# Two fused layers on one core: the first norm worked on the spectrum, image loads moved into room the scans leave, spectral matrices built beside the last image, a norm's factor by logarithm and exponential

## The chip, the cores and the metric

The kernel runs on one core of one Trainium2 chip. The metric is the time on the device, in microseconds, of one execution; the median of several runs is given, with the lowest and the highest. The profile is of one further execution. A core has several engines with an instruction stream each: PE (TensorE, matrix products into PSUM), DVE (VectorE), ACT (ScalarE, table functions), POOL (GpSimd) and SP (SyncE, used here to start transfers; ACT can start them too). They run side by side and wait for one another by semaphores. SBUF is the memory on the core with 128 partitions, PSUM the one that PE writes to, DRAM the memory outside.

## The reference, cut to what matters

The input `x` has the shape (4, 48, 48, 128): four images of 48 by 48 with 128 channels. Two layers are applied, each as a group norm, an inner function and a residual:

```python
x = x + _L0_conv_ref(_gn(x), ...)     # selective scan in four directions
x = x + _L1_conv_ref(_gn(x), ...)     # attention with Fourier layers
```

Inside layer 0, after a projection, a 3 by 3 convolution per channel and a SiLU, this runs for four directions of each image, over 2304 positions, 256 channels and 16 states:

```python
h = h * exp(dt_l * A) + (dt_l * u_l) * B_l
y = einsum('bkdn,bkn->bkd', h, C_l)
...
y = (y - mu) * rsqrt(var + 1e-05) * norm_g + norm_b      # layer norm over channels
y = y * silu(z);  out = einsum('bhwd,cd->bhwc', y, out_proj_w)
```

Layer 1 sees the group-normed result as 4 x 48 single pictures of 48 by 128 (a batch of 4, 48 time steps T; H is 48, W the 128 channels). Its first step is an instance norm of every picture (mean and variance over H and W). Keys, queries and values are each a spectral convolution of that (a real 2-d Fourier transform, a product with learned weights on the low frequencies, the inverse) plus a skip; 32 heads attend over the 48 time steps; then come a projection with a spectral convolution, two more instance norms, and two spectral layers `wM0` and `wM1`, with a GELU between them.

## The kernel before, in words

**Layer 0** (`layer0`, from line 53). The 128 partitions hold channels, in two halves (`NF` = 2). Four images, four directions in the order 0, 2, 1, 3, five chunks each (four of 480 positions, one of 384) and 16 states make 1280 steps. A step is spread over the engines by a table of lags (`LAGS`, line 544), and every instruction in it goes through `on.`, which keeps the order in which the program was written on each engine. In a step PE copies B's row to all partitions (`pb`), DVE multiplies it with `du` (`db`, in three of four states; in the fourth POOL does it from a row that SP has loaded, `bbc`), ACT makes `da` by two exponentials, DVE runs the scan (`h`), POOL multiplies by C (`hc`, whose rows SP loads two states at a time as `cbc`), and PE adds `hc` up over the states (`yp`). ACT carries the last state of a chunk to the next (`carry`).

Once per step `piece()` (line 528) hands out one piece of side work: the projection of the next direction (`project`), the projection and convolution of the next image (`front`, started in the third chunk of an image's first direction, and by none in the last image), or the end of a chunk (`back`, lines 343 to 390). `back` is one of this for every chunk of an image's last direction: 20 in all, of which the last stands behind the last scan. It subtracts the mean over channels, squares (ACT), sums (PE, `pv`), takes the square root (ACT) and the reciprocal (DVE) for the factor `rs`, makes the gate `z` (PE, ACT's Identity and SiLU), multiplies (POOL), projects (PE, `po` and `pr`) and writes the chunk of x1 to DRAM:

```python
on.scalar.activation(rs[:, 0:n], pv[:, 0:n], AF.Sqrt, bias=eps)          # L363
...
    if f == 0:
        on.vector.reciprocal(rs[:, 0:n], rs[:, 0:n])                     # L371
...
on.vector.tensor_mul(xo[:, 0:n], po[:, 0:n], rs[:, 0:n])                 # L381
```

**Layer 1** (`layer1`, from line 642). Instructions written with `nc.` are placed by the framework's scheduler in each engine's order; those with `on.` keep the written order. The stages:

1. x1 is read back as `xa`, four images side by side on the free axis (L744). Weights for values and projection become `dgt` in DRAM (L762 to 793), every head's block 16 times over. `spectral_weights` (948 to 979) makes two sets of 32 matrices of 96 by 96 from `wM0` and `wM1` and two constant Fourier matrices: POOL multiplies (`wih`), PE multiplies (`psw`), ACT copies to one buffer (`spw`), SP stores to DRAM (`sp_d`).
2. Group-norm statistics (ACT copies a block, DVE's bn_stats reads the copy), the affine on all of `xa` (L999), then `first_norm` (695 to 719): the mean by 48 entries of 384 columns on PE with a 128 by 128 matrix of constants (`pm_in`), the subtraction on DVE and POOL, squares on ACT, the variance on PE (`pv_in`), the factor `r`.
3. `prepare` (823 on) makes selectors, and the products of query and key weights (`w_q`, `w_k`, `g_qk`) from some 90 small loads on SP. `forward_w` (721 to 734) transforms along W, multiplies by `r` on the way out of PSUM, and writes `da_x` to DRAM, from which `load_a2` (736) reads it with H on the partitions. PE transposes the pictures (`xnt`) and applies selectors (`psel`, `pplain`, L1041 to 1057).
4. Scores and softmax (L1119 to 1171).
5. Attention times values (L1219 to 1276): for two pairs of images and four groups k of frequencies, three slices q of time steps and four groups g of heads. SP loads `xrep` (16 transfers of 16 partitions for each q, L1227) and `grep` from `dgt` (one transfer for each g, at q = 0, L1235); ACT copies a part of `grep` to PSUM (`gp`), DVE and POOL multiply (`v`, `v3`), PE sums up (`acc`). Buffers: four of `grep` (pool `pg`, L1183), two of `xrep`, `v` and `v3` (pool `p2`, L1182).
6. The rest of layer 1 in two interleaved strands (`Strand`, from 1341), which read `sp_d` back.

Of the kernel before, what the change touches and what calls it, by code (L numbers as in the profile page):

```python
# [53 lines left out]
def layer0(ctx, tc, io, x1_dram):  # L54
# [14 lines left out]
    small = ctx.enter_context(tc.tile_pool(name="l0_small", bufs=2))  # L69
    ps_s = ctx.enter_context(tc.tile_pool(name="l0_pss", bufs=1, space=PSUM))  # L70
    ps_b = ctx.enter_context(tc.tile_pool(name="l0_psb", bufs=1, space=PSUM))
    ps_a = ctx.enter_context(tc.tile_pool(name="l0_psa", bufs=1, space=PSUM))
# [207 lines left out]

    def load_dt(b, k):
        w_dt = two.tile([32 + R, D], F32, tag="w_dt", name=f"w_dt{b}_{k}")
        nc.sync.dma_start(w_dt[32 : 32 + R], io["dt_proj_wT"][k])
        return w_dt
# [58 lines left out]
    def back(b, s, n, yb, x, w, wb):  # L343
# [19 lines left out]
        on.scalar.activation(rs[:, 0:n], pv[:, 0:n], AF.Sqrt, bias=eps)  # L363
        for f in range(NF):
# [5 lines left out]
            if f == 0:  # L370
                on.vector.reciprocal(rs[:, 0:n], rs[:, 0:n])  # L371
# [214 lines left out]
    for j, chunks in enumerate(directions):  # L586
# [9 lines left out]
        for m, c in enumerate(chunks):  # L596
            c.carry = carries[j % 2]
            for i in range(N):
                if k == ORDER[0] and b + 1 < B and m > 1 and coming is None and not any(g in later for g in backs):
                    coming = front(b + 1, images[b + 1])  # L600
                    later.append(coming)
                if i in (N // 2 + 3, N // 2 + 6):
# [13 lines left out]
    while later:  # L616
        piece()

# [24 lines left out]
def layer1(ctx, tc, io, x1_dram, out):  # L643
# [5 lines left out]
    nc = tc.nc  # L649
    img = ctx.enter_context(tc.tile_pool(name="l1_img", bufs=1))  # L650
    const = ctx.enter_context(tc.tile_pool(name="l1_const", bufs=1))
    small = ctx.enter_context(tc.tile_pool(name="l1_small", bufs=2))
    dram = ctx.enter_context(tc.tile_pool(name="l1_dram", bufs=1, space=DRAM))
# [9 lines left out]

    ident = load("ident1", [128, 128], io["c_ident"])
    gmat = load("gmat1", [128, 128], io["c_group"])
    fw = load("fw", [128, 66], io["c_FW"])
    fh = load("fh", [96, 96], io["c_FH"])
    fhi = load("fhi", [96, 96], io["c_FHI"])
    ih = load("ih", [96, 96], io["c_IH"])
    eps = const.tile([128, 1], F32, name="eps1")  # L670
    nc.gpsimd.memset(eps, 1e-5)
    mean_m = const.tile([128, 128], F32, name="mean_m")
    nc.gpsimd.memset(mean_m, 1.0 / (H * W))
    n_g = everywhere("n_g", io["L1_norm_g"], 6)
# [3 lines left out]

    turn = [0]

    def either():
        turn[0] += 1
        return nc.gpsimd if turn[0] % 3 == 0 else nc.vector
# [8 lines left out]
    def per_image(t, n=HB):  # L692
        return t[:, None, :].to_broadcast([128, n, BT])

    def first_norm(psum, work, x):

        pm = psum.tile([128, 512], F32, tag="st", name="pm_in")
        for q in range(H // 2):
            nc.tensor.matmul(pm[:, 0 : 2 * BT], mean_m, x[:, 2 * q : 2 * q + 2], start=(q == 0), stop=(q == H // 2 - 1))  # L699
        m = small.tile([128, BT], F32, tag="in_m", name="in_m")  # L700
        nc.scalar.copy(m, pm[:, 0:BT])
        nc.vector.tensor_add(m, m, pm[:, BT : 2 * BT])
        pv = psum.tile([128, 512], F32, tag="st", name="pv_in")
        for q in range(0, H, HB):
            d = x[:, q : q + HB]
            either().tensor_sub(d, d, per_image(m))
            sq = work.tile([128, HB, BT], F32, tag="blk", name=f"sq_{q}")
            nc.scalar.activation(sq, d, AF.Square)
            for j in range(0, HB, 2):
                nc.tensor.matmul(  # L710
                    pv[:, 0 : 2 * BT], mean_m, sq[:, j : j + 2], start=(q + j == 0), stop=(q + j == H - 2)
                )
        r = small.tile([128, BT], F32, tag="in_r", name="in_r")
        nc.scalar.copy(r, pv[:, 0:BT])
        nc.vector.tensor_add(r, r, pv[:, BT : 2 * BT])
        nc.scalar.activation(r, r, AF.Sqrt, bias=eps)
        nc.vector.reciprocal(r, r)
        nc.vector.tensor_scalar(r, r, n_g[:, 0:1], None, ALU.mult)
        return r

    def forward_w(psum, work, src, r, name):


        da = dram.tile([2, 33, H, BT], F32, name=f"da_{name}")
        for q in range(0, H, HB):
            a = work.tile([66, HB, BT], F32, tag="blk", name=f"a_{name}{q}")
            for j in range(0, HB, 2):
                p = psum.tile([128, 512], F32, tag="mm", name=f"pa_{name}{q}_{j}")
                nc.tensor.matmul(p[0:66, 0 : 2 * BT], fw, src[:, q + j : q + j + 2], start=True, stop=True)
                nc.vector.tensor_mul(  # L730
                    a[:, j : j + 2], p[0:66, 0 : 2 * BT].rearrange("p (a t) -> p a t", t=BT), per_image(r, 2)[0:66]
                )
            nc.sync.dma_start(da.rearrange("c k h t -> (c k) h t")[:, q : q + HB], a)
        return da
# [7 lines left out]
    xa = img.tile([128, H, BT], F32, name="xa")  # L742
    for b in range(B):
        dmas[b % 2].dma_start(xa[:, :, b * T : (b + 1) * T], x1_dram[b])  # L744

    pair_t = [img.tile([128, H, 128], F32, tag=f"p{p}", name=f"xnt{p}") for p in range(2)]
    sp_d = [dram.tile([96, 32, 96], F32, name=f"sp_d{i}") for i in range(2)]
# [4 lines left out]
    dgt = dram.tile([4, NH, 16, 3 * NC], F32, name="dgt")  # L752
    with ExitStack() as pw:
# [30 lines left out]
        for k in range(4):  # L784
            gt = q1.tile([NH, 3, NC], F32, name=f"gtt{k}")
            for c in range(3):
# [4 lines left out]
            nc.sync.dma_start(  # L791
                dgt[k], gt.rearrange("h c n -> h (c n)")[:, None].to_broadcast([NH, 16, 3 * NC])
            )
# [29 lines left out]
    def prepare():  # L823
# [30 lines left out]

        cqk = pe.tile([T, NH], F32, name="cqk")
        nc.vector.tensor_mul(cqk, ws_q[0:T], ws_k[0:T])
# [975 lines left out]
```

## Time and profile before

| what | us |
|---|---|
| median of 3 runs (lowest, highest) | 5088.06 (5079.85, 5090.88) |
| profiled execution, its time | 5084.95 |
| profiled execution, its span | 5083.1 |
| DVE busy in the span | 4225.4 (83%) |
| PE busy | 4214.9 (83%) |
| POOL busy | 4033.8 (79%) |
| ACT busy | 2911.3 (57%) |

In the profile "L50" is the line of the helper that records all `on.` instructions, so those groups are told apart by their tiles. A group's line gives engine, operation, output and inputs with their sizes (partitions x elements), the count, then the busy time in us and the mean of one in ns, then the idle time of the engine just before them and what ended it. In the chain of work that ended last each row is a start, a length and what it was; "issue" is time in which nothing in the profile was waited for, and a q behind an engine's name (SPq, ACTq) is its sequencer, which starts transfers. Stretches of the span in this case: layer 0 ends with the issue of its last x1 write at 4213.10, the scores start at 4411.76, attention times values runs from about 4547 to 4810, and the strands begin at 4812.36.

### The profile page before, as it was taken

How to read it: one execution, taken by the hardware profiler on the slowest of the kernel's cores; microseconds unless marked ns; L12 is line 12 of the kernel's file. 1: busy time of each engine (PE TensorE's matmuls, PEld its weight loads, DVE VectorE, ACT ScalarE, POOL GpSimd, SP SyncE). 2: the span in 40 equal slices, each digit the busy share in tenths (PEclk: the TensorE clock that was granted, in tenths of full speed). 3: DMA queues.
4: the chain of work that ended last, by engine and by line, in shares of the span. 5: the costliest groups of instructions: out<-in, count | busy, mean ns of one | idle time of the engine just before them, and what ended most of it. 6: DMA issues, size and time to landing. Idle time of an engine off the chain costs nothing. (4 is left out here: it accounts for less than half of the span.)

```text
span 5083.1 us, 44364 instructions
## 1 busy us (share of the span) xinstructions
PE 4214.9 (83%) x12344; PEld 1897.5 (37%) x12344; DVE 4225.4 (83%) x2908; ACT 2911.3 (57%) x6446; POOL 4033.8 (79%) x2219
## 2 busy tenths in 40 slices
PE   6889898888798988887989888878787785888876
PEld 2334333333343333333433333333333332453343
DVE  3689998989899989898999898999999983356536
ACT  3666566666565666665656666656656552223334
POOL 4589998988899989798999898899999872346531
PEclk9989999999899999998999999999899986989977
DMA  1223233323233333232333332333233226236546
GB/s 54 72 88 101 93 113 92 101 91 96 93 107 105 104 93 100 88 99 92 106 103 107 91 102 84 99 105 103 99 104 94 93 71 127 64 81 176 166 99 152
DMA packets 276767, 509.25 MB, mean 100 GB/s; under 512 B 100602, under 2 KB 185434, under 8 KB 276326
## 3 DMA queue, kind: packets, MB, share of 16 engines
q1 hardware_dynamic: 265318, 502.61, 32.8%
q10 hardware_dynamic: 11200, 3.81, 0.5%
q8 instruction: 97, 1.59, 0.1%
q14 instruction: 152, 1.25, 0.1%
HBM read 462.58 MB, written 43.72 MB: 100 GB/s over the span
## 5 line engine op out<-in xcount | busy, mean ns | idle before, releaser
L50 POOL TENSOR_TENSOR hc<-h,cbc 128x960 f32<-128x960 f32 (+1 forms) x1280 | 2719.2, 2140 | 461.9 <-DVE h L50 337.4
L50 DVE TENSOR_TENSOR_SCAN h<-da,carry,db 128x961 f32<-128x961 f32 (+1 forms) x1280 | 2702.3, 2130 | 121.2 <-ACT carry L50 86.8
L50 ACT ACTIVATE da<-dt,a_neg 128x480 f32<-128x480 f32 (+1 forms) x2560 | 1661.2, 649 | 1247.4 <-DVE h L50 1201.6
L50 PE MATMUL yp<-hc,ident 128*128 128x480 f32 (+1 forms) x5120 | 2279.6, 573 | 6.8 <-POOL hc L50 6.6
L50 PEld LDWEIGHTS yp<-hc,ident 128*128 128x128 f32 x5120 | 1008.0, 199 | 1428.5 <-issue 1022.4
L50 DVE TENSOR_TENSOR db<-du,pb 128x960 f32<-128x960 f32 (+1 forms) x960 | 1063.1, 1107 | 210.6 <-PE pb L50 155.5
L50 PE MATMUL pb<-bs,pick 112*128 112x480 bf16 (+1 forms) x960 | 360.6, 376 | 400.9 <-DVE db L50 399.2
L50 POOL TENSOR_TENSOR db<-du,bbc 128x960 f32<-128x960 f32 (+1 forms) x320 | 688.5, 2152 | 0.0
L50 PE MATMUL pc<-pad,cdiag 128*128 128x480 f32 (+1 forms) x630 | 283.2, 561 | 9.0 <-ACT pad L50 9.0
L1248 POOL TENSOR_TENSOR v<-grep,xrep 128x768 f32<-128x768 f32 x96 | 174.2, 1821 | 111.2 <-PE acc L1252 64.0
L50 POOL TENSOR_TENSOR du<-dt,xc 128x480 f32<-128x480 f32 (+1 forms) x160 | 204.9, 1281 | 37.1 <-ACT dt L50 37.1
L1252 PE MATMUL acc<-v,attn_c 128*64 128x384 f32 x1152 | 212.8, 511 | 25.8 <-POOL v L1248 15.8
L1244 DVE TENSOR_TENSOR v<-gp,xrep 128x1536 f32<-128x1536 f32 x96 | 165.3, 1754 | 82.4 <-PE acc L1252 36.2
L50 PE MATMUL px<-xc,w_xp 128*112 128x480 f32 (+1 forms) x320 | 215.6, 761 | 17.0 <-ACT xc L50 13.3
L50 ACT COPY db<-carry 128x1 f32<-128x1 f32 x1280 | 226.0, 177 | 5.4 <-DVE db L50 2.1
L50 PEld LDWEIGHTS <-pick 112*128 112x128 bf16 x960 | 97.9, 102 | 331.8 <-issue 307.6
L50 ACT ACT_TABLE_LOAD x146 | 187.3, 1283 | 25.5 <-PE gv_g L50 13.8
L50 PE MATMUL pd<-xd,w_dt 8*128 8x480 f32 (+1 forms) x320 | 167.9, 605 | 38.6 <-ACT bs L50 24.6
L50 ACT COPY carry<-h 128x2 f32<-128x2 f32 x1024 | 192.7, 188 | 0.0
L50 PEld LDWEIGHTS pc<-pad,cdiag 128*128 128x128 f32 x630 | 121.9, 194 | 142.3 <-issue 114.8
L50 PE MATMUL yp<-y,ident 128*128 128x480 f32 (+1 forms) x240 | 166.4, 823 | 0.2
L1252 PEld LDWEIGHTS acc<-v,attn_c 128*64 128x64 f32 x1152 | 88.2, 141 | 146.6 <-issue 63.4
(367 smaller groups left out, 3183.2 us busy)
## 6 DMA issues: line engine op xcount, KB each, us to landing
cbc<-cd SPq DMA_DIRECT2D x512, 480.0 KB
bbc<-cd SPq DMA_DIRECT2D x256, 240.0 KB
cbc<-cd SPq DMA_DIRECT2D x128, 384.0 KB
xrep<-dxt SPq DMA_DIRECT2D x384, 72.0 KB
grep<-dgt SPq DMA_DIRECT2D x32, 576.0 KB
bbc<-cd SPq DMA_DIRECT2D x64, 192.0 KB
dgt<-gtt SPq DMA_DIRECT2D x4, 2304.0 KB
x<-in_xT SPq DMA_DIRECT2D x16, 288.0 KB
```

The costliest lines, as they stand in the source:

```text
L50: return lambda *args, **kw: self._tc.keep_in_program_order(emit(*args, **kw))
L1244: nc.vector.tensor_mul(v, gp[:, None, :, 0:NC].to_broadcast([128, 2, 2, NC]), x[:, :, 0:2])
L1248: nc.gpsimd.tensor_mul(v3, r[:, 2:3].to_broadcast([128, 2, NC]), x[:, :, 2])
L1252: nc.tensor.matmul(acc[c][64 * b : 64 * b + 64, 0:NC], attn_c[:, 2 * pair + b, g, q], v[:, b, c] if c < 2 else v3[:, b], start=first, stop ...
```

## The change

**In layer 0.** `back` takes the logarithm on ACT in place of the square root, and an exponential with the scale -0.5 on ACT in place of DVE's reciprocal. `spectral_weights` is gone from layer 1; a generator `matrices()` makes the same two sets of matrices as side work of `piece()`, started in the third chunk of the last image's first direction. It works in the room of `cdiag` (the convolution's diagonals), with ACT for the products with the weights and the copies, PE for two transposes and 64 products, SP for 11 loads and 32 stores. The pool `ps_a` is opened ahead of two others. Layer 0 is called from inside layer 1 (`io["first"]`), whose pools `imgs`, `const` and `small` are then taken from the other side of SBUF.

**Between the layers.** x1 is read back by SP into `x_in`, two images side by side in each of two tiles, three images whole and the fourth in five chunks.

**In layer 1's front.** bn_stats reads `x_in`. The group norm's affine is no longer applied to `xa` ahead of the first norm: it is folded into the matrices for the mean (`a_m`) and the transform (`fwa`, `fwb`), and into the centring, which writes `xa`. Means and variances are 24 matmuls each with 32 columns of weights, one group of 32 output partitions for each image, and are spread to all partitions by `g_of`. `forward_w` no longer waits for the norm; it takes turns with it. The mean over H at frequency 0 is subtracted and the factor `r0` is multiplied in behind `load_a2`, on `a2`. `da_x` is written from ACT's queue, and half of the evacuations are ACT's. The products of query and key weights are a function `products()`, written behind `load_a2`, with their DVE instructions in written order.

**In the later stages.** `dgt` is stored once for each head; `grep` is read by eight transfers of 72 KB, each of one row to 16 partitions, for one of 576 KB. `ih` is loaded ahead of the strands.

```diff
@@ back
-        on.scalar.activation(rs[:, 0:n], pv[:, 0:n], AF.Sqrt, bias=eps)
+        on.scalar.activation(rs[:, 0:n], pv[:, 0:n], AF.Ln, bias=eps)
...
-                on.vector.reciprocal(rs[:, 0:n], rs[:, 0:n])
+                on.scalar.activation(rs[:, 0:n], rs[:, 0:n], AF.Exp, scale=-0.5)
@@ matrices (new), called from the loop over steps
+        for n in range(2):
+            for k in range(0, 32, 2):
+                for c in range(2):
+                    for i in range(2):
+                        on.scalar.activation(m[3 + 2 * c + i], m[2], AF.Copy, scale=w[:, n, c, k + i : k + i + 1])
+                    if c == 0:
+                        yield FREE
+                p = side(f"psp{n}_{k}")
+                for c in range(2):
+                    on.tensor.matmul(p[0:96, 0:192], m[c], room[:, (3 + 2 * c) * 96 : (5 + 2 * c) * 96],
+                                     start=(c == 0), stop=(c == 1))
+                yield
+                on.scalar.copy(room[:, 7 * 96 : 9 * 96], p[0:96, 0:192])
+                nc.sync.dma_start(sp_dram[n][:, k : k + 2].rearrange("p k m -> p (k m)"), room[:, 7 * 96 : 9 * 96])
+                yield FREE
...
+                if k == ORDER[0] and b + 1 == B and m > 1 and coming is None and not any(g in later for g in backs):
+                    coming = matrices()
+                    later.append(coming)
@@ layer1: loads
-    for b in range(B):
-        dmas[b % 2].dma_start(xa[:, :, b * T : (b + 1) * T], x1_dram[b])
+    x_in = [imgs.tile([128, 2, H, T], F32, tag=f"p{p}", name=f"x_in{p}") for p in range(2)]
+    for b in range(B):
+        for s, n in CHUNKS if b == B - 1 else [(0, L)]:
+            h = slice(s // T, (s + n) // T)
+            nc.sync.dma_start(x_in[b // 2][:, b % 2, h], x1_dram[b][:, h])
@@ first_norm
+        def sums(p, what, weight):
+            for q in range(0, H, HB):
+                for b in range(B):
+                    nc.tensor.matmul(p[32 * b : 32 * b + 32, 0 : HB * T], weight(b), what(b, q),
+                                     start=(q == 0), stop=(q == H - HB))
...
+                nc.vector.scalar_tensor_tensor(d, x[b // 2][:, b % 2, q : q + HB], aff[:, 0, b : b + 1],
+                                               m[:, b, None, :].to_broadcast([128, HB, T]), ALU.mult, ALU.add)
+                nc.scalar.activation(sq[:, b], d, AF.Square)
+                nc.tensor.matmul(pv[32 * b : 32 * b + 32, 0 : HB * T], mean_m, sq[:, b], ...)
@@ layer1: behind load_a2
+        nc.tensor.matmul(p0[0:H, 0:BT], over_h, a2[0:H, 0], start=True, stop=True)
+        nc.vector.tensor_sub(a2[0:H, 0], a2[0:H, 0], p0[0:H, 0:BT])
+        for s in range(0, 33, 11):
+            v = a2[:, s : s + 11]
+            nc.vector.tensor_mul(v, v, r0[0:96, None, :].to_broadcast([96, 11, BT]))
...
+        products()
@@ dgt and grep
-            nc.sync.dma_start(dgt[k], gt.rearrange("h c n -> h (c n)")[:, None].to_broadcast([NH, 16, 3 * NC]))
+            nc.sync.dma_start(dgt[k], gt.rearrange("h c n -> h (c n)"))
...
-                            nc.sync.dma_start(r.rearrange("p c n -> p (c n)"),
-                                dgt[k, 8 * g : 8 * g + 8].rearrange("h r n -> (h r) n"))
+                            for i in range(8):
+                                nc.sync.dma_start(r[16 * i : 16 * i + 16].rearrange("p c n -> p (c n)"),
+                                    dgt[k, 8 * g + i].partition_broadcast(16))
```

## The prediction

> **What bounds the kernel now.** I read the busy shares first: DVE 4225.4 us and PE 4214.9 us (both 83%), POOL 4033.8 us (79%), ACT 57%. These are means over two very different halves, so the next view is the busy time by stretch; the columns are stretch, length, then busy time of PE, PE weight loads, DVE, ACT and POOL, the clock, the DMA share and GB/s.
>
> ```profile
> 1000.00:2000.00 1000.00, 862.76 (x2103) 377.13 (x2103) 934.31 (x590) 643.94 (x1461) 908.94 (x466) 0.96 0.31 98
> 4213.00:4412.00 199.00, 134.22 (x760) 69.31 (x760) 64.89 (x137) 61.06 (x127) 45.23 (x88) 0.80 0.54 113
> 4547.00:4812.00 265.00, 223.26 (x1221) 95.33 (x1220) 175.22 (x118) 85.28 (x118) 170.61 (x94) 0.96 0.57 163
> ```
>
> Layer 0 (to 4213) is bound by DVE, with POOL 25 us in 1000 behind it. From 4213 to the scores at 4412 no engine is full: a chain of waits. From 4547 to 4812 (attention times values) PE leads, but SP feeds it. The groups kept apart by shape give layer 0's step:
>
> ```profile
> L50 DVE TENSOR_TENSOR_SCAN h<-da,carry,db 128x961 f32<-128x961 f32 x1024 | 2244.3, 2210 | 97.3 <-ACT carry L50 86.8 <-ACT db L50 7.5 <-POOL hc L50 2.9
> L50 DVE TENSOR_TENSOR db<-du,pb 128x960 f32<-128x960 f32 x768 | 880.9, 1147 | 192.2 <-PE pb L50 149.2 <-DVE h L50 1.4
> L50 DVE RECIPROCAL ws<-ws 128x480 f32<-128x480 f32 x16 | 50.1, 3132 | 4.9 <-ACT ws L50 4.9
> L50 POOL TENSOR_TENSOR hc<-h,cbc 128x960 f32<-128x960 f32 x1024 | 2259.4, 2221 | 415.8 <-DVE h L50 305.0 <-issue 41.9 <-PE yp L50 38.5
> L50 POOL TENSOR_TENSOR db<-du,bbc 128x960 f32<-128x960 f32 x256 | 571.5, 2232 | 0.0
> ```
>
> Four steps cost DVE 4 x 2.210 + 3 x 1.147 = 12.28 us, POOL 4 x 2.221 + 2.232 + du's share 0.66 (2 x 1.326 in 16 steps) = 11.78. DVE leads by 4%; POOL's idle time ends with DVE's h. DVE's own waits (100 to 4180: total, times, longest) show what it is late for otherwise:
>
> ```profile
> DVE db L50 <- PE pb L50: 101.1, 82, 5.9
> DVE h L50 <- ACT carry L50: 86.8, 27, 4.8
> ```
>
> (po follows with 40.8 in 16.)
>
> The chain that ended last, between the last x1 write (issued 4213.10) and the scores (start, us, what):
>
> ```profile
> 4219.79 22.39 DMA xa<-x
> ...
> 4266.30 5.66 DVE xa L999 x4
> ...
> 4272.01 18.12 PE pm_in L699 x48
> ...
> 4316.77 1.87 DMA sp_d<-spw
> ...
> 4371.31 8.26 DMA a_x<-da_x
> ```
>
> Load, affine, mean, variance (13.18 for pv_in at 4299), sixteen spectral stores one after the other, transform, reload: all serial. Last, SP in the attention stage: its timeline (start, us, line, count; one stretch of each kind), then its waits.
>
> ```profile
> 4573.57 29.26 SPq L1227 DMA_DIRECT2D xrep<-dxt  x48
> 4602.95 2.78 SPq L1235 DMA_DIRECT2D grep<-dgt  x4
> ```
>
> ```profile
> SPq L1227 <- DVE v L1244: 25.3, 14, 5.9
> SPq L1227 <- DMA grep<-dgt: 24.7, 16, 3.0
> ```
>
> In the chain there an xrep issue takes 0.42 us and 0.04 between two, in runs of 16: SP's issuing is on the path already. 416 issues x 0.46 = 192 us of 265.
>
> **What the Trainium skill says.** "ScalarE: Activation LUTs", section "What ACT_TABLE_LOAD costs": about 1283 ns a load, 186 ns + 0.833 ns per column an activation, some 93 ns more with a pointer operand; the trace agrees (load 1283; a 480-column exponential with pointers 665). Its section on table sets says that ln and exp share a set. In the instruction order of the changed kernel as built, the loads per layer norm stay at four: Ln takes a set that is not the Exp's, in Sqrt's place. "DMA: Bandwidth & Descriptors", "Issuing engines are not separate DMA queues", calls initiation time "usually small relative to the DMA itself"; at 0.46 us per 72 KB this trace says otherwise. "TensorE: Matmul & The Clock Gate", Part 3, gives 2.38x for three column groups at once; here 158 psel matmuls of 32 columns ran in 6.69 us, 42 ns each, against 378 ns for a 128-wide pm_in.
>
> **The change part by part.**
>
> A, the norm's factor. DVE loses 16 x 3.13 + 4 x 2.53 = 60.2 us of reciprocals; one is in the tail, hidden by the gate's matmuls and Identity. The other 19 stand between scans, DVE back to back around them (idle 3 us in 2141 to 2260), so at most 57 us. Per chunk of 16 steps with a layer norm DVE goes from 54.7 to 51.6 us, POOL has 49.3: POOL does not take over. What is late next is pb, the carry and po; I give a fifth to them: -45 (bounds -56, and -15 if they take most). ACT gains 20 x 0.586 = 12 us, at 64% busy.
>
> B, matrices in the last image. ACT: 128 products (96 columns, pointer scale: 0.36 less 0.09 overlap) 34 us, 32 copies of 192 columns 11 us; PE 64 matmuls 22 us at pc's rate; SP 11 loads and 32 stores. They go one piece per step over some 98 steps of 3.2 us, where the earlier images run the next image's convolution: image periods are 1012, 1014 and, without it, 987 us. A convolution costs 26 us with far more in it; I take +5 (0 to +15). Without that cover it would be 46 us of ACT.
>
> C, the PSUM pool's order: nothing, no instruction differs.
>
> Tail of the last layer norm: ACT's chain is as long (Exp for the reciprocal), but DVE's statistics of images 0 and 1 stand ahead of the product and the sum that make x1: up to two 0.48 us bn_stats ahead of each, +0.8 (0 to +3).
>
> D and E, from x1 to the scores. On before's clock: last x1 issue 4213.9; write and the reload of that chunk, two DMAs of 2 to 4.5 us, end at 4221. The rest must be in by then: SP's first loads (sp, w_wQ) now write into room that the last hc reads (4183), and x_in's first awaits the tail's second Identity (about 4197); behind them on SP stand some 30 small loads, 8 us by 0.25 each, and 3.5 MB of images, 18 us at the 197 GB/s of the xa load: about 4219, just covered. Then the last statistics, behind w_p's load (4.5 us) in DVE's order, 4226; group affine 7 (8.6 now, with a wait), 4233. The affine on xa (5.66) is gone. Mean: 24 matmuls at 0.378 are 9.1 us serial, 3.8 at the skill's 2.38; the 36 transposes for dgt (4.28 per 18) interleave and the spread back takes a reduction and four matmuls: 17 together, 4250. Then centring, squares, variance and transform side by side: DVE 24 x 0.475 + 12 evacuations x 0.55 = 18 us (estimated by 1.0417 ns a column + 75 ns, "Vector Engine (DVE) Microarchitecture Reference", 5.2; the trace's 960 columns take 1.147, this gives 1.075), ACT 24 x 0.51 + 12 x 0.55 = 19; with start 23: 4273. da_x write 3.5, reload 8.3 and issues 5: 4290. From there the selectors take what they take now, 4385.4 to 4411.8, so 26: scores at 4316. Beside it DVE scales a2 (3 x 2.27), then products(): 1.74 and some 30 x 0.25, then a DMA: 4309, so just hidden; were it not, every us counts. Gone: 16 spectral stores of 2.46 us, which held the stretch 4316 to 4354, and 9.4 MB of dgt writes. In all 4412 to 4316 = -96, the tail included (bounds -60 and -110).
>
> F, dgt once. Writes fall from 9.4 to 0.6 MB (counted in E). But 32 grep issues become 256: SP has 640 issues in a stage of 265 us, and the greps that wait for POOL's v to free their buffer hold up the xrep loads queued behind them, for which DVE, POOL and PE then wait. At 0.465 that is 298; a pair-and-k period needs 80 x 0.465 = 37.2 us and takes about 35.6 now, so SP becomes the bound: +33 if its waits vanish, +104 if all stay; at the broadcast loads' 0.32 + 0.04 (cbc, 480 KB) it is 274, +9. The lane waits behind the 576 KB greps (24.7) should go; waits for v stay in part. I take +40.
>
> G, ih loaded at the Strands' start: one 37 KB load ahead of the first pe_p, +2 (0 to +2.5).
>
> Sum: -45 + 5 - 96 + 40 + 2 = -94 on the profiled 5084.95 (span 5083.1 and 1.85 around it): 4991. The median of the runs stands 3 us above the profiled one: 4994.
>
> **The rivals.**
> 1. SP does not bind in the attention stage (issues 0.36, lane waits gone): F +10, 4964. For: cbc's 0.32. Against: xrep, of the same 16 partitions as the new greps, 0.42. Chance 0.22.
> 2. DVE's place in layer 0 is taken at once: pb and carry waits grow by what the reciprocals leave, A -15: 5024. For: 101 and 87 us of these waits already. Against: they are few, and DVE runs unbroken through the layer norm's stretch. Chance 0.13.
> 3. The front does not shorten as laid out: the products or the SP queue (some 90 small weight loads ahead of what the scores need) end last, E -50: 5040. Chance 0.10.
> 4. Slower: SP in the attention stage. Without F the change gives 134 us; 144 more are needed, 0.64 us for each of 224 issues with all present waits kept, or 0.96 with none. No issue in the trace is near it (0.32 to 0.46), unless greps of one row read by 16 partitions land late and each lane waits. 5110. Chance 0.04.
> 5. The sum as made, 4994, its own range 4975 to 5015: 0.48. Three in a hundred are left for no change by some mixture.
>
> **How the numbers follow.** 0.2%, 10 us, is about what a measurement of this kernel can tell from no change. Rivals 1, 2, 3 and the sum are faster: 0.93; within 0.03, slower 0.04. The range from 4950 (rival 1 with A at its bound) to 5045 (rival 3) leaves under 2 in 10.
>
> **What would show it.** A: no RECIPROCAL of 480 columns on DVE, image periods shorter by 13 to 14 us; DVE's waits for pb and carry up by under 15 us. B: the last period longer than the shortened 973 by 5. E: xnt and scores some 100 us after the last x1 issue, no psw or sp_d in that chain. F: SP's issues back to back from the first xrep to the last, 0.42 each, stage near 305. The prediction is wrong if the stage from the first xrep to the Strands stays under 275, if image periods shorten by under 5 us, or if scores start over 130 us behind x1.

## The result and the profile after

The changed kernel takes 5081.39 us (median of 12 runs, 5077.52 to 5087.41), the kernel before 5079.57 (12 runs). The ratio is 0.9999, 95% interval 0.9991 to 1.0008: no difference. 4994 had been forecast, with 4950 to 5045 as the range. The profiled execution has a span of 5078.8 us, against 5083.1 before. Cut at the same events in both traces, the span shows where the 94 us went:

| stretch (events) | before | after | difference | forecast |
|---|---|---|---|---|
| layer 0, first to last scan | 4097.8 | 4090.9 | -6.9 | -45 + 5 |
| last scan to the issue of the last x1 write | 36.2 | 38.8 | +2.6 | +1 |
| to the first score product (f, DVE) | 198.7 | 111.6 | -87.1 | -97 |
| to the first xrep issue | 117.8 | 119.4 | +1.6 | 0 |
| attention times values, to the first pe_p | 284.4 | 375.2 | +90.8 | +40 + 2 |
| the strands, to the end | 269.1 | 263.9 | -5.2 | 0 |

The front gave nine tenths of what was forecast, layer 0 a sixth, and the attention stage took more than the front had given. (By these events the attention stage was 284.4 us long before; the 265 us of the prediction begin at 4547, after the first transfers.) The strands took between 261 and 269 us in the twelve other runs too, in no order that follows the edits, so their 5 us are not put down to the change.

The busy time by stretch of the changed kernel (same columns as before), for the front and the attention stage:

```profile
4209.00:4320.00 111.00, 87.76 (x729) 46.46 (x730) 53.99 (x141) 50.27 (x115) 4.79 (x37) 0.85 0.30 67
4440.00:4815.00 375.00, 262.52 (x1313) 116.39 (x1314) 182.38 (x136) 89.68 (x124) 175.84 (x111) 0.82 0.62 127
```

DVE and POOL do the same work as before (182 us for 181, 176 for 176, counted from the first xrep to the strands in both), in 375 us for 284, so they wait longer. SP's timeline there, one period's greps and the xrep loads behind them (a period is one pair of images and one k; there are eight):

```profile
4492.18 16.38 SPq L1338 DMA_DIRECT2D grep<-dgt  x32
4508.67 27.78 SPq L1329 DMA_DIRECT2D xrep<-dxt  x48
```

4 issues in 2.8 us have become 32 in 16.4, and the 48 of xrep, with the waits between them, take about what they took (27.8 for 29.3). This period is 44.4 us; the mean of the eight is 46.9. The share of each line in the chain of waits, first for the kernel before (4547 to 4812), then for the changed one (4440 to 4810), shows SP moving from an eighth of the chain to 44%, while PE's acc falls from a third to an eighth:

```profile
by line: PE acc L1252 33.2%; POOL v L1248 20.0%; SPq L1227 11.8%; DMA xrep<-dxt 10.7%; DVE v L1244 9.1%; DMA grep<-dgt 7.2%; issue 3.5%; SPq L1235 0.9%; PE pz L1270 0.9%; DVE zt L1265 0.4%; DVE zt L1263 0.4%; DVE s L1264 0.4%; ACT z L1273 0
```

```profile
by line: SPq L1329 23.0%; SPq L1338 21.1%; DMA xrep<-dxt 14.8%; PE acc L1355 13.3%; POOL v L1351 10.8%; DMA grep<-dgt 10.5%; issue 6.0%; DVE zt L1368 0.2%; DVE zt L1366 0.2%; DVE s L1367 0.2%; POOLq L1351 0.1%; PE pz L1373 0.1%; DVEq L1366 
```

The front's chain in the changed kernel: the mean's sum takes 12.5 us from its first product to the next step where it took 18.1, no sp_d is in it, and the reload ends at 4279.09, with the transposes and selectors (41 us) between it and the scores.

```profile
4222.88 2.77 PE pm_in L779 x10
...
4251.60 3.51 DMA da_x<-a_x
...
4272.42 6.67 DMA a_x<-da_x
...
4300.29 9.70 PE psel L1143 x158
```

In layer 0 the scans and db products cost what they cost; DVE's waits (100 to 4160: total, times, longest) have grown in the two places that were largest before:

```profile
DVE db L50 <- PE pb L50: 124.1, 110, 5.9
DVE h L50 <- ACT carry L50: 109.6, 35, 5.7
DVE ws L50 <- PE po L50: 24.7, 15, 3.6
DVE h L50 <- ACT db L50: 22.9, 7, 6.2
DVE h L50 <- POOL hc L50: 19.4, 8, 2.9
```

The kernel before has 101.0, 86.8, 38.0, 31.4 and 2.9 in these rows. With two smaller rows (yb and da) the sum goes from 268 to 313 us. That is 45 of the 57 us that the reciprocals among the scans took; some of it is due to the matrices.

### The profile page after: what moved, and what is told of

Its sections match the earlier page's. It is cut to its first block, busy times and chain, and to the rows that moved or that the text cites. A ratio compares the mean times of both kernels' runs of the same rounds, so it can differ in the third digit from the quotient of the medians.

```text
span 5078.8 us, 45097 instructions
## 1 busy us (share of the span) xinstructions
PE 4197.2 (83%) x12436; PEld 1892.6 (37%) x12436; DVE 4164.5 (82%) x2905; ACT 2954.4 (58%) x6620; POOL 3993.7 (79%) x2193
## 4 chain that ended last, share of the span: by engine, by line
DVE 17%; PE 13%; issue 8%; ACT 7%; SPq 3%; DMA 3%; POOL 3%; DVEq 0%; ACTq 0%; POOLq 0%
DVE h L50 13%; PE yp L50 3%; ACT da L50 3%; DVE db L50 3%; SPq L1329 2%; SPq L1338 2%; ACT L50 1%; DMA xrep<-dxt 1%; PE acc L1355 1%; PE sc L1228 1%; POOL db L50 1%; PE pi_p L50 1%; POOL v L1351 1%; DMA grep<-dgt 1%; ACT dt L50 1%
## 5 line engine op out<-in xcount | busy, mean ns | idle before, releaser
L50 POOL TENSOR_TENSOR hc<-h,cbc 128x960 f32<-128x960 f32 (+1 forms) x1280 | 2717.7, 2137 | 455.2 <-DVE h L50 331.0
L50 DVE TENSOR_TENSOR_SCAN h<-da,carry,db 128x961 f32<-128x961 f32 (+1 forms) x1280 | 2702.6, 2129 | 157.2 <-ACT carry L50 109.6
L50 ACT ACTIVATE da<-dt,a_neg 128x480 f32<-128x480 f32 (+1 forms) x2560 | 1661.1, 649 | 1177.6 <-DVE h L50 1131.8
L50 PE MATMUL yp<-hc,ident 128*128 128x480 f32 (+1 forms) x5120 | 2263.8, 569 | 4.8 <-POOL hc L50 4.6
L50 PEld LDWEIGHTS yp<-hc,ident 128*128 128x128 f32 x5120 | 1001.1, 197 | 1375.2 <-issue 1017.7
L50 DVE TENSOR_TENSOR db<-du,pb 128x960 f32<-128x960 f32 (+1 forms) x960 | 1063.7, 1108 | 234.8 <-PE pb L50 179.5
L50 POOL TENSOR_TENSOR db<-du,bbc 128x960 f32<-128x960 f32 (+1 forms) x320 | 687.9, 2150 | 0.0
L50 PE MATMUL pb<-bs,pick 112*128 112x480 bf16 (+1 forms) x960 | 358.1, 373 | 373.3 <-DVE db L50 371.7
L1355 PE MATMUL acc<-v,attn_c 128*64 128x384 f32 x1152 | 235.1, 562 | 90.0 <-POOL v L1351 87.8
L50 PE MATMUL pc<-pad,cdiag 128*128 128x480 f32 (+1 forms) x630 | 282.3, 559 | 7.3 <-ACT pad L50 7.3
L50 POOL TENSOR_TENSOR du<-dt,xc 128x480 f32<-128x480 f32 (+1 forms) x160 | 204.5, 1278 | 37.9 <-ACT dt L50 37.9
L50 PE MATMUL px<-xc,w_xp 128*112 128x480 f32 (+1 forms) x320 | 216.6, 765 | 16.9 <-ACT xc L50 13.3
L50 ACT COPY db<-carry 128x1 f32<-128x1 f32 x1280 | 225.8, 176 | 6.4 <-DVE db L50 3.2
L50 PEld LDWEIGHTS <-pick 112*128 112x128 bf16 x960 | 97.5, 102 | 330.5 <-issue 307.0
L50 ACT ACT_TABLE_LOAD x147 | 188.6, 1283 | 27.3 <-PE gv_g L50 13.9
L50 PE MATMUL pd<-xd,w_dt 8*128 8x480 f32 (+1 forms) x320 | 168.1, 605 | 39.2 <-ACT bs L50 27.7
L50 ACT COPY carry<-h 128x2 f32<-128x2 f32 x1024 | 192.7, 188 | 0.0
L1345 ACT COPY gp<-grep 128x768 f32<-128x768 f32 x96 | 76.5, 802 | 195.3 <-DVE v L1347 119.1
L50 PEld LDWEIGHTS pc<-pad,cdiag 128*128 128x128 f32 x630 | 121.3, 193 | 139.4 <-issue 113.3
```

Source lines behind the costliest of these rows:

```text
L50: return lambda *args, **kw: self._tc.keep_in_program_order(emit(*args, **kw))
L1345: nc.scalar.copy(gp[:, :, 0:NC], r[:, 0:2])
L1355: nc.tensor.matmul(acc[c][64 * b : 64 * b + 64, 0:NC], attn_c[:, 2 * pair + b, g, q], v[:, b, c] if c < 2 else v3[:, b], start=first, stop ...
```

## The experiments

Two questions were put: what lengthens the attention stage, and what keeps the reciprocals' time in layer 0. The ratios are against runs of the kernel before on the same chip. Stages are cut at the events of the table above, in one profile of each run. How far single profiles differ can be seen where the code is the same: the front with dgt stored 16 times took 136.6 to 138.6 us in five runs, and the first image of layer 0 took 1069.2 to 1075.7 us in seven.

### The attention stage

**First run: part F undone in the changed kernel** (wide greps: one transfer of 576 KB each, and dgt stored 16 times).

```diff
-    dgt = dram.tile([4, NH, 3 * NC], F32, name="dgt")
+    dgt = dram.tile([4, NH, 16, 3 * NC], F32, name="dgt")
...
-                            for i in range(8):
-                                nc.sync.dma_start(... dgt[k, 8 * g + i].partition_broadcast(16))
+                            nc.sync.dma_start(... dgt[k, 8 * g : 8 * g + 8].rearrange("h r n -> (h r) n"))
```

> The changed kernel with part F undone: dgt stored 16 times, grep again one transfer of 576 KB, 32 in all. Theory 1 (SP's queue of 640 issues sets the attention stage): the stage from the first xrep issue to the strands' first pe_p falls from 375 us to about 284, and the kernel to 5081 - 91 + 0 to 20 for the 9.4 MB of dgt writes that come back in the front, so 4990 to 5010. Theory 2 (the small broadcast reads land late) expects the same here. Theory 3 (the stage is long because it starts earlier or for another part of the change): the stage stays near 375 and the time near 5080.

5012.55 us, ratio 0.9878 (0.9862 to 0.9895). The stage is 283.0 us, as before the change. The front is 138.6 us in place of 111.6: the 9.4 MB of dgt writes cost it 27. So F as a whole costs the changed kernel 92 - 27 = 65 us, and without it the change is worth 63.

**Second run: the same 256 transfers from ACT's queue.**

```diff
-                                nc.sync.dma_start(
+                                nc.scalar.dma_start(
                                     r[16 * i : 16 * i + 16] ..., dgt[k, 8 * g + i].partition_broadcast(16))
```

> The changed kernel with its 256 grep transfers of 72 KB issued from ACT's queue in place of SP's, nothing else. Theory 1 (SP's issues): SP has 384 left, ACT takes 256 x 0.46 = 118 us beside 85 us of work in the stage; the stage falls to 285 to 310, the kernel to 4990 to 5015. Theory 2 (late landing of small broadcast reads): the stage stays near 375, the kernel near 5080.

5130.87 us, ratio 1.0109 (1.0094 to 1.0124); the stage is 427.5 us. Both theories missed. ACT's timeline shows why this run does not test SP:

```profile
4566.15 0.80 ACT L1345 COPY gp<-grep 128x768 f32<-128x768 f32 x1 [8.71 <-DMA grep<-dgt]
4566.16 5.92 ACTq L1338 DMA_DIRECT2D grep<-dgt  x8
4573.96 0.80 ACT L1345 COPY gp<-grep 128x768 f32<-128x768 f32 x1 [7.01 <-DMA grep<-dgt]
```

ACT issues one grep's eight transfers, and the copy that needs them stands next in its order. Of the 7.0 us without a copy shown last, about 5 go into the issues and 1.9 into waiting for the last of them to land; only behind the copy do the next eight begin. In this order the transfers do not run ahead of the engine that consumes them.

**Third run: eight transfers from SP, each from 16 separate rows** (dgt 16 times, the source `dgt[k, 8 * g + i]`).

> The changed kernel with dgt stored 16 times, and grep still read by eight transfers of 72 KB from SP, but each from 16 separate rows, so that no row is read by several partitions. Theory 1: the stage stays near 375 us, the kernel at 5080 to 5100 (the dgt writes are back). Theory 2, as far as the rereading of one row is what is slow: the stage falls to about 300.

5103.12 us, ratio 1.0056 (1.0041 to 1.0071); the stage is 371.3 us. Sixteen partitions reading one row is not what is slow: with distinct rows it is 4 us shorter. Theory 2 falls, as far as the rereading goes. The kernel as a whole is longer than the changed one because the 16-fold writes are back in its front (136.6 us).

**Fourth run: F alone in the kernel before** (the first run's diff the other way round).

> The kernel before with part F alone (dgt stored once, eight grep transfers from SP). Theory 1: the stage grows from 284 to about 375 us, the dgt writes that saturated the DMA engines beside the load of xa go; together 5080 + 91 - (0 to 20) = 5150 to 5170. Theory 3 (F alone is harmless, the stage is long only in the changed kernel): 5060 to 5090.

5159.25 us, ratio 1.0162 (1.0147 to 1.0177). The stage is 375.4 us, the front 183.7 for 198.7. F costs 91 us in this stage with none of the other parts there; its saved writes give back 15 in the old front.

**Twelfth run: four transfers of 144 KB for each grep** (dgt stored 16 times).

```diff
+                            for i in range(4):
+                                nc.sync.dma_start(r[32 * i : 32 * i + 32] ...,
+                                    dgt[k, 8 * g + 2 * i : 8 * g + 2 * i + 2].rearrange("h r n -> (h r) n"))
```

> The changed kernel with dgt stored 16 times, and each grep read in four transfers of 144 KB: 128 issues, between the 32 of the first run (stage 283 us) and the 256 of the third (371 us), the bytes the same. SP then has 512 issues x 0.465 = 238 us. Theory 1a (the stage grows only once SP's issues fill it, near 570 issues): 283 to 290 stays, kernel 5010 to 5020. Theory 1b (every added issue stands on the chain in any case, because the greps wait for buffers and the xrep loads queue behind them): about 283 + 88 x 96 / 224 = 321, kernel 5045 to 5055.

5056.27 us, ratio 0.9955 (0.9938 to 0.9972); the stage is 328.7 us. With the same bytes read, 32, 128 and 256 grep issues give 283.0, 328.7 and 371.3: 0.48 us for each of the first 96 added, 0.33 for each of the next 128. SP's issues fill the stage at neither of the first two counts (193 and 238 us by 0.465). So it is not the filling of SP that counts, as the prediction had it: the stage grows from the first added issue on. Added up from the three traces, the issues of xrep and grep take 174.9, 203.5 and 261.3 us, and the rest of the time from the first of them to the last is 88.8, 103.4 and 88.1: what is added is not taken out of SP's waits. What these runs vary is the number and the size of the transfers together. In the twelfth run's chain the landings of grep and xrep have grown as well as SP's issues (from 4470 to 4740 they have 34.5% and 27.3%, for 16.0% and 14.6% in the first run), so how much of the price is the issue and how much the landing of a smaller transfer is not separated.

**Eighth run: the other side of it.** The time slices are stored twice over, so that xrep is 8 transfers of 32 partitions, with wide greps as in the first run.

```diff
-                        for i in range(8):
-                            nc.sync.dma_start(x[16 * i : 16 * i + 16, b] ..., dxt[2 * pair + b, k, q * 16 : q * 16 + 16])
+                        for i in range(4):
+                            nc.sync.dma_start(x[32 * i : 32 * i + 32, b] ..., dxt[2 * pair + b, k, q].rearrange("r p n -> (r p) n"))
```

> The changed kernel with wide greps and dgt stored 16 times (as in the first run), and with the time slices (dxt) stored twice over, so that xrep comes in 8 transfers of 32 partitions in place of 16 of 16: SP's issues in the attention stage fall from 416 to 224, the bytes read stay, 3.5 MB more are written during the scores. Theory 1 (SP's issues set this stage, in the kernel before too): the stage falls from 283 us to 225 to 250, the kernel from 5012 to 4960 to 4985. Theory 2 (bytes or landing of the reads set it): 283 stays, 5010 to 5020.

The stage is 256.7 us for 283.0, a little above the range of theory 1; theory 2 falls. That is 0.14 us for each of the 192 issues taken away. The share of each line in its chain there:

```profile
by line: PE acc L1360 44.0%; POOL v L1356 22.9%; DMA xrep<-dxt 9.9%; DVE v L1352 9.4%; issue 3.3%; SPq L1335 2.3%; PE pz L1378 2.2%; ACT gp L1350 1.0%; DVE zt L1373 0.9%; DVE zt L1371 0.9%; DVE s L1372 0.9%; DMA iw<-in_c_IW 0.9%; ACT z L138
```

SP is gone from it (2.3%) and PE leads. The kernel as a whole took 5057.31 us (0.9954, 0.9939 to 0.9969), slower than the first run, because the stretch from the scores to the first xrep issue grew from 117.2 to 192.7: the planner (the scheduler that orders the instructions written with `nc.`), given six stores in place of one, put 152 of the 256 matmul records that make the slices (pxt) behind the last score; in the changed kernel it is 8.

**Tenth run: dgt stored once, and multiplied by a copy within DRAM beside the scores.**

> The changed kernel with wide greps, dgt first stored once and then multiplied by a copy from DRAM to DRAM that stands behind the reload of the spectrum, while the scores run. Theory: the 9.4 MB of dgt writes cost the front 27 us (scores 138.6 us behind the last x1 write with them, 111.6 without), so they come back: 5012 - 27 = 4985 (4980 to 4995), with the attention stage at 284. If the front was short for another reason, 5005 to 5015.

5064.70 us, ratio 0.9971 (0.9957 to 0.9984). The front is 112.4 us, so the 27 us did come back, and the attention stage is 281.2. But the scores to the first xrep take 200.4 us, again from the planner's order: 232 of the 256 pxt records stand behind the last score, where each group of eight waits for a copy, a sum and the store of the group before. Its trace, the matmuls for the slices, with the scores already over at 4406:

```profile
L1194 PE MATMUL pxt<-fh,a_x x256: 246/367/397, 4286.7 to 4513.3; 96*48 96x96 f32 x128
L1231 PE MATMUL sc<-f,qs x384: 486/486/902, 4319.5 to 4403.3; 128*64 128x384 f32 x192
```

In the changed kernel the last pxt starts at 4427.6 and the last score at 4424.5. The expectation of the total failed; that of the two stages held.

### Layer 0

**Fifth run: part A alone in the kernel before** (the two lines of the change's diff in `back`).

> The kernel before with part A alone: logarithm and exponential on ACT for square root and reciprocal, four table loads per layer norm as before. Theory 1 (ACT's table loads take the place of the reciprocal, which had covered them): layer 0's last x1 write comes 8 to 14 us earlier, as the first three images show in the changed kernel (3.3 each), so 5066 to 5072. Theory 2 (what is lost in the changed kernel is lost to its other parts, A alone is worth what the reciprocals took): 45 us, 5035.

5072.07 us, ratio 0.9977 (0.9970 to 0.9983): about 12 us. First to last scan is 4084.2 us for 4097.8. Theory 2 falls: about four fifths of the reciprocals' 57 us are lost with no other part of the change there.

**Sixth run: two of the four table loads of each layer norm taken away, the reciprocal left.** The root is left out of the result.

```diff
-        on.scalar.activation(rs[:, 0:n], pv[:, 0:n], AF.Sqrt, bias=eps)
+        on.scalar.activation(rs[:, 0:n], pv[:, 0:n], AF.Identity, bias=eps)
```

> The kernel before with the square root replaced by Identity, which is in Exp's table set: two table loads per layer norm less (2.57 us of ACT each time), the reciprocal stays. The root is left out, so the factor is 1/(var + eps) in place of its root. Theory 1 (reciprocal and table loads cover each other in the same steps): little, 0 to 15 us faster, 5065 to 5080. Theory 3 (ACT's loads alone bound these steps): 30 to 45 us, 5035 to 5050.

5078.10 us, ratio 0.9991 (0.9983 to 0.9999); first to last scan 4087.6 us. The trace has 110 table loads for 149. Theory 3 falls: ACT's loads do not bind alone either.

**Seventh run: reciprocal and two loads taken away, with nothing left out.** Part A, and behind each SiLU, Softplus and group-norm root of layer 0:

```diff
+        on.scalar.preload_act_table_set("natural_log_exp_and_others")
```

> The kernel before with part A, and with the table set that holds both logarithm and exponential loaded by hand behind every SiLU, Softplus and group-norm root of layer 0, so that neither Ln nor the next Exp needs a load: two loads per layer norm, 112 in all for 150. Theory 1 (each hides the other): much more than the sum of the two before, 35 to 50 us faster, 5030 to 5045. Theory 4 (POOL, or PE's pb and po, take DVE's place in these chunks at once): not much over part A alone, 10 to 20 us, 5060 to 5070.

5052.00 us, ratio 0.9939 (0.9926 to 0.9951): about 31 us, short of the 35 to 50 forecast by theory 1 and beyond theory 4's 20. First to last scan is 4060.3 us, and 112 loads are left. Against before, A gives 13.6, the loads 10.2, and both 37.5, more than their sum of 23.8. Without the first image, which differs between profiles of the same code, it is 10.5, 4.8 and 31.6; the ratios of the whole kernel give 12, 5 and 31. So both together are worth about twice their sum.

One place of the 19 shows it step by step: the third chunk of the third image's last direction, the same five scans in each run. DVE's timeline of the kernel before:

```profile
3042.07 2.22 DVE L50 TENSOR_TENSOR_SCAN h<-da,carry,db 128x961 f32<-128x961 f32 x1
3044.20 3.13 DVE L50 RECIPROCAL ws<-ws 128x480 f32<-128x480 f32 x1
...
3055.36 2.22 DVE L50 TENSOR_TENSOR_SCAN h<-da,carry,db 128x961 f32<-128x961 f32 x1 [1.51 <-ACT carry L50]
...
3058.54 2.21 DVE L50 TENSOR_TENSOR_SCAN h<-da,carry,db 128x961 f32<-128x961 f32 x1
```

and of the changed kernel:

```profile
3038.05 2.21 DVE L50 TENSOR_TENSOR_SCAN h<-da,carry,db 128x961 f32<-128x961 f32 x1
3040.90 1.16 DVE L50 TENSOR_TENSOR db<-du,pb 128x960 f32<-128x960 f32 x1 [0.64 <-PE pb L50]
...
3045.72 1.16 DVE L50 TENSOR_TENSOR db<-du,pb 128x960 f32<-128x960 f32 x1 [1.54 <-PE pb L50]
...
3051.37 2.22 DVE L50 TENSOR_TENSOR_SCAN h<-da,carry,db 128x961 f32<-128x961 f32 x1 [2.36 <-ACT carry L50]
...
3054.55 2.21 DVE L50 TENSOR_TENSOR_SCAN h<-da,carry,db 128x961 f32<-128x961 f32 x1
```

From the first to the last scan shown it is 16.47 us before and 16.50 after: of 3.13 us of reciprocal, nothing came back. The fifth run, with part A alone, has 16.50 as well. With the two loads gone and the reciprocal kept it is 14.85 (sixth run), and DVE has no idle time left between the five; with both gone it is 13.49. The seventh run's timeline of DVE:

```profile
3022.95 2.22 DVE L50 TENSOR_TENSOR_SCAN h<-da,carry,db 128x961 f32<-128x961 f32 x1
...
3033.26 2.22 DVE L50 TENSOR_TENSOR_SCAN h<-da,carry,db 128x961 f32<-128x961 f32 x1 [1.32 <-ACT carry L50]
...
3036.44 2.21 DVE L50 TENSOR_TENSOR_SCAN h<-da,carry,db 128x961 f32<-128x961 f32 x1
```

The chain of waits of the changed kernel at the place (`ACT L50` without a tile is a table load):

```profile
3036.60 1.28 ACT L50
...
3038.61 1.86 PE pz L50 x2
...
3040.87 3.01 PE yp L50 x4
3043.88 1.61 PE pz L50 x2
...
3046.20 1.28 ACT L50
...
3048.51 1.28 ACT L50
```

Between the first load and the scan that waits for the carry lie 14.77 us; in the kernel before, from its load at 3040.62 to its scan at 3055.36, 14.74. The row runs through two engines: a load and the logarithm (or root) on ACT, 6.9 us on PE with the gate's two products (pz) and the steps' own products between them, then on ACT the gate's second Identity, a load, SiLU, a load and the exponentials of the scan, all in written order. Three of the four loads lie on it, 3.8 us. It is as long with the logarithm as with the root, and in the kernel before the reciprocal ran beside its part on PE (3044.20 to 3047.33). That the other 18 places go the same way is not shown one by one; the sums above are of all.

### What the parts make together

**Ninth run: the changed kernel with wide greps and the one table set** (the diffs of the first and the seventh run).

> The changed kernel with wide greps and dgt stored 16 times, and with the one table set for Ln and Exp loaded by hand, two table loads per layer norm less. If what these loads cost is the same in the changed kernel as in the kernel before with part A, layer 0 gains 24 us more: 5012 - 24 = 4988 (4980 to 4996). If the work of the matrices or something else of the change fills the place, 5005 to 5012.

4992.37 us, ratio 0.9826 (0.9812 to 0.9841), the shortest of all runs: 1.7% below the kernel before, and within the 4980 to 4996 expected. First to last scan is 4073.1 us here and 4063.5 in the eleventh run, whose layer 0 is the same: 17.8 and 27.4 less than in the changed kernel, on both sides of the 24. Without the first image it is 11.8 and 16.0, for 21.1 between the fifth and the seventh run: the last image, with the matrices, gains least (997.0 and 993.5 us, for 986.7 in the seventh run).

**Eleventh run: this with the late copies and the halved xrep.**

> The three together: one table set, late copies of dgt with wide greps, xrep in half the transfers. If they add: 5012 - 24 - 27 - 27 to 52 = 4910 to 4935.

5056.49 us, ratio 0.9953 (0.9936 to 0.9969). Front 112.4 and attention stage 258.2 us are what the parts gave; the scores to the first xrep take 237.3, by the planner's order again. The 4910 to 4935 stay open: no run kept the slices between the scores with these edits.

## Why the prediction was wrong, by its own steps

**A, the norm's factor: -45 said, -10.5 to -13.6 measured alone.** The step that failed is "POOL does not take over ... I give a fifth to" the other waits: about four fifths went to them. It asked which engine is next by busy time (POOL, 49.3 against 51.6 us in a chunk), and ACT at 64% busy was not looked at within a layer norm's steps. At the place shown the bound is a row of work through ACT and PE that the scan needs, with 3.8 us of table loads in it. The reciprocal lay in its shadow, or it in the reciprocal's. Rival 2 had the size (-15), with the pb and carry waits it named growing by 46 us where under 15 had been said, and it was given 0.13. That the count of loads stays at four had been read in the order, and was used only to price ACT's work, not to ask what it stops.

**B, the matrices: +5 said.** The last image takes 995.2 us in the changed kernel and 988.4 with A alone: +6.8; beside the one table set it is +10.3 and +6.8 (ninth and eleventh run against the seventh). Right in kind and within its bounds.

**C** could not be told apart from nothing. **The tail**: +2.6 for +0.8, within its bounds.

**D and E, the front: -96 said with the tail, -84.5 measured with it.** The structure came as laid out: no serial spectral stores, statistics beside the load, the transform beside the norm. That the total lies so near is in part luck. 27 of the 87 are F's saved writes, which the sum had counted without a number; without them D, E and the tail gave 57.5 (first run), just short of the bound of -60. Counted from the last x1 issue, the reload ended about 6 us earlier than forecast, but from there to the scores it took 41 us and not the 26 of "the selectors take what they take now": most transposes (pxn) stand behind the reload (the kernel before had begun 76 of 96 records ahead of it, the changed one 12), the mean at frequency 0 does too, and the selectors took longer (9.70 us for 158 against 6.69, at a granted clock of 0.76 against 1.00). Single readings were off too. The 48 records of pm_in in the kernel before are 24 written products, so the new 24 are 18.1 us one after the other and not 9.1; in four groups side by side they took about 8 of the 12.5 us measured. (The 42 ns of psel and the 378 of pm_in are for 192 and 384 columns.) The centring's 24 instructions took 607 ns each in the mean, not the 475 estimated from the Trainium skill's "Vector Engine (DVE) Microarchitecture Reference", section 5.2; the measurement decides.

**F, grep in eight: +40 said, +91 measured, twice (375.2 against 284.4 us, and 375.4 in the kernel before).** This is the term that turned the sum. The step that failed is "SP becomes the bound: +33 if its waits vanish". It treated SP as an engine with 73 us to spare that has to be filled first. The chain of the kernel before already showed runs of sixteen issues on it, and the twelfth run shows that the first 96 added issues cost 0.48 us each with SP still unfilled. The end "+104 if all stay" was the better reading: from the first issue to the last, SP's issues took 259.4 us for 173.7 before, and the rest of that time 94.5 for 91.3. The reason given for it in the prediction is not the one that the changed kernel shows. Its greps no longer wait for their buffers (8.5 us in the kernel before, no such row now). What waits is the first xrep of each next period, which needs one of the two xrep buffers back from DVE, with that period's greps behind it on the queue:

```profile
SPq L1329 <- DVE v L1347: 36.8, 7, 5.5
SPq L1329 <- DMA xrep<-dxt: 11.1, 58, 0.3
```

The waits for v were 25.3 us before. The forecast that the waits behind the wide greps would go was right in part: those behind grep transfers fell from 24.7 to 9.3 us on SP, but 11.1 of short waits behind xrep transfers stand in their place. Whether a third xrep buffer, or another order on the queue, would bring these 36.8 us back was not tried. The lower clock of PE in this stage (below) is not what lengthened it, by the chain of waits: acc's part of the chain fell from 88 to 49 us.

**G**: from the last v to the first pe_p 10.5 us for 9.2: +1.3.

With A at 13.6 and F at 91 the prediction's own sum is -13.6 + 5 - 96 + 91 + 2 = -12, within 8 us of the -4.3 measured. Each of the two values lay near an end named in the text (-15 and +104); both fell on the bad side, and the range, made of one rival at a time, did not reach to both. That both fall together was left to the three in a hundred for "some mixture". Of the marks set for being wrong, the image periods hit: 1010.4 for 1013.8, 3.4 us shorter and not 13. A small slip besides: 384 issues at 0.465 and 256 at 0.36 are 271, so rival 1's end is +6 and not +9.

The Trainium skill's "ScalarE: Activation LUTs", in its section on table sets, says that ln followed by exp needs one load. As built, this program did not get that: with Ln in Sqrt's place the trace has 150 loads for 149. It held in the seventh, ninth and eleventh runs, where the common set was loaded by hand (112 loads).

## What to carry to other kernels

Before an instruction is taken out because its engine is the busiest, look at the steps around it in the timeline of each other engine: what is late there by the same time can fill the gap, and then the pair has to be removed together (here 12 and 5 us apart, 31 together). Where a chain of waits already shows runs of transfer issues on a queue, price each added issue near its full duration, not at what is left after the queue is full. Here that was 0.33 to 0.48 us from 416 issues up; from 224 to 416, where PE led the chain, it was 0.14. And a saving on bytes that multiplies the transfers has to be set against that price where they are issued: here 27 us of writes against 91.

## What the runs showed of the hardware and had not been expected

- Sixteen partitions reading one row of 4.6 KB were about as fast as sixteen partitions reading sixteen rows: the stage took 375.2 and 371.3 us.
- Issued from the engine that consumes them, the same 256 transfers made the stage 427.5 us, for 375.2 from SP.
- The clock granted to TensorE in the attention stage was 0.82 in the changed kernel and 0.93 in the kernel before (0.96 in the shorter cut that the prediction shows); the acc matmuls took 562 ns in the mean for 511. PE was busy for 70% of the stage at 0.82 and for 84% at 0.93; the second run had 64% and 0.78, the twelfth 77% and 0.85, the eighth 84% and 0.97. An emptier PE went with a lower clock; which of the two follows from the other is not shown.
